# A two-block AdaLN transformer on one core: ScalarE's squares of the projected banks move behind VectorE's two products

## The chip, the cores and the metric

The kernel runs on one core of one Trainium2 chip. The metric is device time in microseconds (us) from the start to the end of one execution, lower is better. The kernel before was run three times: 1238.51, 1242.51 and 1245.01 us, median 1242.51 us.

A core has five engines that run side by side and wait for each other by semaphores: TensorE (PE in the profile, with its weight loads as PEld), VectorE (DVE), ScalarE (ACT), GpSimd (POOL) and SyncE (SP, which here issues DMAs). Each of them works through its own list of instructions in order. TensorE writes its results to PSUM, which has 8 banks of 128 partitions x 512 fp32 numbers; here each matmul result of a step takes one bank.

## The reference

The reference is two blocks of a transformer with adaptive layer norm. The change lies in the last part of the second block, a small "local attention" transformer of two layers on 4 sequences of 1024 tokens with 128 channels, 8 heads of 64. For each layer:

```
h  = shift_token(x)                     # half the channels come from the token before
q, k, v = h @ Wqkv                      # 128 -> 3 x 512, 8 heads of 64
q, k = l2norm(q) * q_scale, l2norm(k) * k_scale      # each head's 64 numbers by their length
q, k = rotary_xpos(q, k)                # x*cos + rotate_half(x)*sin, with a scale by position
a  = softmax(8 * q k^T over the 64 tokens of the window before and the own one)
x  = x + (a v) @ Wo
x  = x + GLU-MLP(layernorm(shift_token(x)))          # 128 -> 2 x 341, gelu, -> 128
```

So for every token and head a length is needed: the root of the sum of 64 squares of q, and the same of k.

## The kernel before, in words

From about 580 us on, the kernel works on the local layers (lines 647 to 1096). Tokens are cut into 64 tiles of 128 (2 layers x 4 sequences x 8 tiles), and one loop goes through them, one step for one tile. In step g the stages of several tiles lie side by side: scores of tile g, projections of tile g+2, transposes of q and k of tile g+1, flips of the probabilities of tile g-2, the products with v of tile g-3, and a piece of the output projection or of the MLP. TensorE's order is written by hand (the loop runs under a manual schedule for PE); for the other engines a tile scheduler orders the instructions from their dependencies and the order of the source text, sets the semaphores, and hands out the buffers of the pools, PSUM's among them: 6 banks in turn for everything of "mid" size, 2 for scores.

One step on PE in order: 32 small matmuls of the scores (L885), projection of q for tile g+2 (L653), the flip of half 0 of tile g-2 (L926), projection of k for tile g+2 (L653), the flip of half 1, the transpose of q of tile g+1 (L845, "turn" with w = 0), the outputs of tile g-3 (L940), the transpose of k of tile g+1 (L845, w = 1), a piece of the MLP, v of tile g-1 (L864), and in one step of four the output projection (L951).

`project` is the function that is changed. It is called twice for a tile, w = 0 for q and w = 1 for k, and each call fills one PSUM bank qk (L653) that three instructions read:

- ScalarE squares it into sq (L656);
- VectorE multiplies it by the cosine table into co (L658);
- VectorE multiplies its swapped halves by the sine table into si (L663).

The framework lets two engines read the same PSUM bank only one after the other, in the order of the source text. Behind them VectorE sums sq over each head into ss (L665, one tile of 16 numbers for q and k together). For w = 1 GpSimd then takes a maximum of ss (L668) and its power -1/2 (L669), adds si to co (L673, for both w), and multiplies the k side by its 1/length (L675). The result is what the transposes (L845) wait for. q's 1/length is used later: VectorE's masking of the scores (L892) takes it as its scale, together with the row minimum. ScalarE's exponentials (L904) follow, eight of them a tile. The division by the sums is done by `over_sums` on tiles of step g-1: a reciprocal (L912) on VectorE, placed behind the copy of the transposed k (L858, kT), then one product for each half (L919), half 0 on GpSimd, half 1 on VectorE. In the MLP pieces, L1004 adds the MLP's result to the stream on VectorE (in the second layer followed by L1006).

Tiles 3 to 7 of the first sequence of the first layer are "light": q's si isn't added on GpSimd, but PE adds it by matmul in the transpose (L849), and half 1's product L919 is done by ScalarE (L917). The first six projections, of tiles 0 to 2, are made earlier, in the last steps of the windowed attention before the local layers (lines 821 and 822).

Of the kernel before, what the change touches and what calls it, by code (L numbers as in the profile page):

```python
# [19 lines left out]
F32 = mybir.dt.float32  # L20
BF16 = mybir.dt.bfloat16
AF = mybir.ActivationFunctionType
# [4 lines left out]
P = 128  # L27
# [9 lines left out]
HEADS, DH, DEPTH = 8, 64, 2  # L37
# [11 lines left out]
def adaln_blocks(ctx: ExitStack, tc: tile.TileContext, a: dict, out: bass.AP):  # L49
    nc = tc.nc  # L50
    pe, act, dve, pool = nc.tensor, nc.scalar, nc.vector, nc.gpsimd
# [11 lines left out]
    def bc(ap, shape):  # L63

        return ap.unsqueeze(len(ap.shape)).to_broadcast(shape)
# [579 lines left out]
    pj = ctx.enter_context(tc.tile_pool(name="pj", bufs=3))  # L645

    def project(l, b, t, w, ps):


        nt = f"{l}_{b}_{t}_{w}"  # L650
        if w == 0:
            late[l, b, t, "ss"] = pj.tile([P, 2, HEADS], F32, tag="ss", name=f"ss_{nt}", bufs=4)
        pe.matmul(ps, lhsT=hs[l, b][:, t * P : (t + 1) * P], rhs=wl[l][0][:, w, :], start=True, stop=True)  # L653
        ph = ps.rearrange("p (h e) -> p h e", e=DH)
        sq = pj.tile([P, HEADS, DH], F32, tag="sq", name=f"sq_{nt}", bufs=2)
        act.activation(sq, ph, AF.Square)  # L656
        co = pj.tile([P, HEADS, DH], F32, tag=f"co{w}", name=f"co_{nt}")
        dve.tensor_tensor(co, ph, abs_[l][:, 0, t, w, :].unsqueeze(1).to_broadcast([P, HEADS, DH]), ALU.mult)  # L658
        si = pj.tile([P, HEADS, DH], F32, tag="si", name=f"si_{nt}", bufs=3)

        ex = bass.AP(tensor=ps.tensor, offset=ps.offset + 32, ap=[ps.ap[0], [DH, HEADS], [-32, 2], [1, 32]])
        sn = abs_[l][:, 1, t, w, :].rearrange("p (i e) -> p i e", i=2).unsqueeze(1).to_broadcast([P, HEADS, 2, 32])
        dve.tensor_tensor(si.rearrange("p h (i e) -> p h i e", i=2), ex, sn, ALU.mult)  # L663
        ss = late[l, b, t, "ss"]
        dve.tensor_reduce(ss[:, w, :], sq, AX.X, ALU.add)  # L665
        if w == 1:

            pool.tensor_scalar(ss, ss, 1.0e-24, None, ALU.max)  # L668
            pool.tensor_tensor(ss, ss, nhalf[:, 0:2].unsqueeze(2).to_broadcast([P, 2, HEADS]), ALU.pow)  # L669
        if w == 0 and light(l, b, t):  # L670
            late[l, b, t, "si"] = si
        else:
            pool.tensor_tensor(co, co, si, ALU.add)  # L673
        if w == 1:
            pool.tensor_tensor(co, co, bc(ss[:, 1, :], [P, HEADS, DH]), ALU.mult)  # L675
        late[l, b, t, "co", w] = co

    def light(l, b, t):

        return (l, b) == (0, 0) and t >= EARLY  # L680
# [5 lines left out]
    with (  # L686
# [107 lines left out]
        for g in range(-1, NG8 + 2):  # L794
            b, t = divmod(g, NT)
            ahead = 0 <= b and b + 1 < B
            if g == -1:
                weights(0, 0)
            when(g + 2, scores)
            when(g + 2, weights)  # L800
            if ahead and t in (2, 4):
                queries(b + 1, t // 2 - 1)
            for after, k, f in ((6, 0, tokens), (8, 0, normed), (11, 1, tokens), (13, 1, normed)):
                if (g - after) % NT == 0 and 0 <= (g - after) // NT < B - 1:
                    f((g - after) // NT, k, "h3")
            for at, k, f in ((1, 0, tokens), (3, 0, normed), (5, 1, tokens), (7, 1, normed)):
                if g == at:
                    f(B - 1, k, "h2")
            when(g - 1, back)
            when(g + 1, flip, (0, 1))  # L810
            when(g + 1, values)
            when(g, outputs)
            when(g + 1, flip, (2, 3))
            if t == 5 and 0 < b <= DEPTH:
                rotary(tab, abs_[b - 1], b - 1)
            if g % 4 == 1 and g > 4:
                project_out((g - 5) // NT, (g - 5) % NT // 4)
            if ahead and t in (3, 5):
                keys(b + 1, t // 2 - 1)

            for i, w in ((0, 0), (0, 1), (1, 0), (1, 1), (2, 0), (2, 1))[max(0, g - NG8 + 6) : max(0, g - NG8 + 7)]:
                project(0, 0, i, w, ps.tile([P, BLK], F32, tag="t", name=f"qk_0_0_{i}_{w}", bufs=2))
# [6 lines left out]
    with (  # L829
# [230 lines left out]
        def project_mid(l, b, t, w):  # L1060
            if (l, b) != (0, 0) or t >= EARLY:
                project(l, b, t, w, pM.tile([P, BLK], F32, tag="mid", name=f"qk_{l}_{b}_{t}_{w}"))
# [161 lines left out]
```

## Time and profile before

| | before |
|---|---|
| three runs, median | 1238.51, 1242.51, 1245.01; 1242.51 us |
| the profiled execution: its time, its span | 1246.33 us, 1244.5 us |
| TensorE clock granted, mean | 0.983 of full speed |
| busy: PE, DVE, ACT, POOL | 1162.8, 878.8, 817.8, 823.3 us |
| the same in the stretch from 800 to 1000 us | 198.49, 173.75, 158.37, 175.65 of 200 us |
| one of the 128 squares (L656, ACT) | 586 ns |
| one cosine product (L658), sine product (L663), head sum (L665), all DVE | 677, 678, 673 ns |
| one add co+si (L673), power (L669), product co*ss (L675), POOL | 1280, 2995, 1044 ns |
| one exponential (L904, ACT), with its accumulator read | 403 + 199 ns, overlapping |
| one masking of a score tile (L892, DVE) | 342 ns |

The durations of an instruction include some overlap with the next of the same engine: in the timeline three VectorE instructions of 0.67 us follow each other every 0.60 us. The busy times are shares of one engine's own time; how long a step takes is read from the start of one block of scores (L885) on PE to the next. The profile's time runs from the span's start.

### The profile page before, as it was taken

To read this page: it belongs to the slowest core of one execution; us is meant where nothing else is said; L and a number is where in the kernel's file an instruction comes from. 1 tells how busy PE (TensorE), PEld (TensorE's weight loads), DVE (VectorE), ACT (ScalarE), POOL (GpSimd) and SP (SyncE) were. 2 spreads that over 40 slices of the span, in tenths; PEclk is the share of its full clock that TensorE was granted. 3 is DMA by queue.
4 is the path that set the end of the run, shared out by engine and by line. 5 is a ranking of instruction groups with operands and counts; after the bars stand their busy time and mean duration, and the time that the engine had idled before them with its cause. 6 is when DMAs were issued, how large, how long until landed. Compare 5 with 4: busy or idle time off the path is not lost.

```text
span 1244.5 us, 34772 instructions
## 1 busy us (share of the span) xinstructions
PE 1162.8 (93%) x13578; PEld 714.7 (57%) x13578; DVE 878.8 (71%) x2798; ACT 817.8 (66%) x2223; POOL 823.3 (66%) x813
## 2 busy tenths in 40 slices
PE   6789999999899999988898999999999999999998
PEld 5644453534476667755665556665555556565564
DVE  5556263452476667666878988898898888998864
ACT  3363373322577677766886788788877887788862
POOL 4436445746334445444889988888899889888840
PEclk8699999999999999999999999999999999999999
DMA  6040404021400000000112111111111111111110
GB/s 179 1 130 8 138 0 132 7 74 63 137 4 4 3 20 14 11 3 3 35 27 48 27 35 26 32 40 27 39 28 34 39 29 45 38 27 31 36 40 26
DMA packets 36136, 51.04 MB, mean 41 GB/s; under 512 B 5850, under 2 KB 17668, under 8 KB 35844
## 3 DMA queue, kind: packets, MB, share of 16 engines
q1 hardware_dynamic: 35540, 48.29, 14.1%
q8 instruction: 107, 1.75, 0.6%
q10 hardware_dynamic: 432, 0.53, 0.1%
q14 instruction: 57, 0.47, 0.1%
HBM read 26.52 MB, written 2.36 MB: 23 GB/s over the span
## 4 chain that ended last, share of the span: by engine, by line
PE 43%; DVE 27%; ACT 18%; POOL 7%; issue 5%; DMA 1%; POOLq 0%; ACTq 0%; SPq 0%; DVEq 0%
ACT pr L904 5%; PE h L489 4%; PE yp L951 4%; DVE pr L892 3%; DVE co L658 3%; PE s L885 3%; DVE si L663 3%; DVE ss L665 3%; PE ptr L735 3%; PE qk L653 3%; POOL u L494 2%; ACT sq L656 2%; PE s L261 2%; PE obank L752 2%; DVE ge L997 2%
## 5 line engine op out<-in xcount | busy, mean ns | idle before, releaser
L904 ACT ACTIVATE pr<-pr,mx 128x128 f32<-128x128 f32 x512 | 200.8, 403 | 88.2 <-DVE mx L892 88.1
L673 POOL TENSOR_TENSOR co<-co,si 128x512 f32<-128x512 f32 x123 | 156.7, 1280 | 79.5 <-DVE si L663 72.2
L669 POOL TENSOR_TENSOR ss<-ss,nhalf 128x16 f32<-128x16 f32 x64 | 191.7, 2995 | 5.3
L892 DVE CUSTOM_DVE_ANT_0 pr<-s,masks,ss 128x128 f32<-128x128 f32 x512 | 144.2, 342 | 42.4 <-PE s L885 42.0
L653 PE MATMUL qk<-wqkv,hs 128*128 128x512 f32 x256 | 137.7, 620 | 4.9 <-ACT pt L737 4.9
L494 POOL TENSOR_TENSOR u<-u,cw 128x512 f32<-128x512 f32 x64 | 81.1, 1271 | 74.4 <-ACT u L492 74.4
L489 PE MATMUL h<-hT,w 128*128 128x512 f32 x256 | 123.8, 605 | 4.0 <-DVE g L496 4.0
L496 DVE TENSOR_TENSOR g<-u,h 128x512 f32<-128x512 f32 x64 | 43.8, 686 | 114.9 <-POOL u L494 114.9
L279 DVE TENSOR_REDUCE mx<-s 128x4 f32<-128x448 f32 x128 | 73.5, 617 | 56.4 <-PE s L270 56.4
L658 DVE TENSOR_TENSOR co<-qk,ab 128x512 f32<-128x512 f32 x128 | 86.7, 677 | 26.0 <-ACT sq L656 26.0
L904 ACT ACTIVATION_READ_ACCUMULATOR pr<-pr,mx 128x1 f32 x512 | 101.7, 199 | 0.0
L492 ACT ACTIVATE u<-h 128x512 f32<-128x512 f32 x64 | 38.2, 598 | 93.2 <-PE h L489 85.7
L926 PEld LDWEIGHTS ptr<-ident,pr 128*128 128x128 f32 x512 | 63.5, 141 | 61.6 <-issue 54.8
L663 DVE TENSOR_TENSOR si<-qk,ab 128x512 f32<-128x512 f32 x128 | 86.8, 678 | 0.0
L489 PEld LDWEIGHTS h<-hT,w 128*128 128x128 f32 x256 | 48.3, 194 | 66.2 <-issue 51.0
L665 DVE TENSOR_REDUCE ss<-sq 128x8 f32<-128x512 f32 x128 | 86.2, 673 | 0.0
L656 ACT ACTIVATE sq<-qk 128x512 f32<-128x512 f32 x128 | 74.9, 586 | 14.8 <-PE qk L653 12.3
L845 PE MATMUL qktr<-ident,co 128*128 128x128 f32 x492 | 76.9, 280 | 6.6 <-POOL co L675 5.3
L885 PEld LDWEIGHTS s<-kT,qT 64*64 64x64 f32 x2048 | 56.8, 134 | 45.6 <-issue 22.1
L919 POOL TENSOR_TENSOR pr<-pr,sm 128x512 f32<-128x512 f32 x64 | 74.7, 1168 | 7.9 <-DVE sm L912 7.9
L885 PE MATMUL s<-kT,qT 64*64 64x128 f32 x2048 | 72.1, 277 | 7.6 <-DVE kT L858 6.1
L737 ACT COPY pt<-ptr 112x512 f32<-112x512 f32 x128 | 72.5, 612 | 8.6 <-PE ptr L735 8.6
(212 smaller groups left out, 2871.2 us busy)
## 6 DMA issues: line engine op xcount, KB each, us to landing
cw<-cd SPq DMA_DIRECT2D x128, 128.0 KB, 3.0
ve<-vs SPq DMA_DIRECT2D x120, 128.0 KB, 2.3
hs<-hT SPq DMA_DIRECT2D x16, 256.0 KB, 3.2
out<-out SPq DMA_DIRECT2D x7, 256.0 KB, 2.7
xin<-in_x SPq DMA_DIRECT2D x3, 512.0 KB, 6.1
w<-in_w SPq DMA_DIRECT2D x3, 512.0 KB, 5.0
wqkv<-in_wqkv SPq DMA_DIRECT2D x2, 768.0 KB, 5.3
ab<-in_tab SPq DMA_DIRECT2D x1, 1024.0 KB, 7.3
```

The lines of the kernel that those rows point to most:

```text
L489: pe.matmul(h, lhsT=w[:, c * P : (c + 1) * P], rhs=hT[b][:, blk(k)], start=True, stop=True)
L494: pool.tensor_tensor(u, u, kept[b, k, "cw"][:, c, :], ALU.mult)
L653: pe.matmul(ps, lhsT=hs[l, b][:, t * P : (t + 1) * P], rhs=wl[l][0][:, w, :], start=True, stop=True)
L656: act.activation(sq, ph, AF.Square)
L658: dve.tensor_tensor(co, ph, abs_[l][:, 0, t, w, :].unsqueeze(1).to_broadcast([P, HEADS, DH]), ALU.mult)
L663: dve.tensor_tensor(si.rearrange("p h (i e) -> p h i e", i=2), ex, sn, ALU.mult)
L665: dve.tensor_reduce(ss[:, w, :], sq, AX.X, ALU.add)
L669: pool.tensor_tensor(ss, ss, nhalf[:, 0:2].unsqueeze(2).to_broadcast([P, 2, HEADS]), ALU.pow)
L673: pool.tensor_tensor(co, co, si, ALU.add)
L885: pe.matmul(S[j][qs, c, :], lhsT=q[rw, c, qs], rhs=k[rw, c, at : at + P], start=True, stop=True)
L892: dve.tensor_tensor_reduce(out=pr[:, c, :], in0=S[j][:, c, :], in1=mk[:, min(t, 1), :], scale=kept[l, b, t, "ss"][:, 0, h : h + 1], scalar ...
L904: act.activation(pr[:, c, :], pr[:, c, :], AF.Exp, bias=mx[:, j, c : c + 1], scale=-1.0, accum_out=sm[:, j, c : c + 1])
```

## The change

Two lines of `project` move: the tile sq and its square on ScalarE are written behind the two products of VectorE instead of ahead of them. Nothing is added and nothing is left out; shapes, pools and buffer counts stay as they are.

```
         pe.matmul(ps, lhsT=hs[l, b][:, t * P : (t + 1) * P], rhs=wl[l][0][:, w, :], start=True, stop=True)
         ph = ps.rearrange("p (h e) -> p h e", e=DH)
-        sq = pj.tile([P, HEADS, DH], F32, tag="sq", name=f"sq_{nt}", bufs=2)
-        act.activation(sq, ph, AF.Square)
         co = pj.tile([P, HEADS, DH], F32, tag=f"co{w}", name=f"co_{nt}")
         dve.tensor_tensor(co, ph, abs_[l][:, 0, t, w, :].unsqueeze(1).to_broadcast([P, HEADS, DH]), ALU.mult)
         si = pj.tile([P, HEADS, DH], F32, tag="si", name=f"si_{nt}", bufs=3)
...
         dve.tensor_tensor(si.rearrange("p h (i e) -> p h i e", i=2), ex, sn, ALU.mult)
+        sq = pj.tile([P, HEADS, DH], F32, tag="sq", name=f"sq_{nt}", bufs=2)
+        act.activation(sq, ph, AF.Square)
         ss = late[l, b, t, "ss"]
         dve.tensor_reduce(ss[:, w, :], sq, AX.X, ALU.add)
```

In the semaphores of the built program this reads, for each of the 128 banks: before, the square waits for PE, the cosine product for the square; after, the cosine product waits for PE, the square for the sine product, and the head sum for the square as before. Since the square of a bank is now its last reader, the next matmul into the same bank waits for the square, and no longer for the sine product.

The scheduler also lays out three engines anew. What most steps hold after the change, in the order of each engine (steps with MLP pieces differ a little):

- ScalarE: the squares come behind the exponentials (exp x3, pt, exp x2, pt, exp x2, square of q, exp, qT, square of k, os), where they came between the first of them.
- VectorE: cosine and sine product of q, then of k, then the head sum of q, kT, the head sum of k, the reciprocal, L919. Before it was cosine, sine, sum of q, cosine, sine, sum of k, kT. In the step in which the MLP's result is added (L1004), that addition too comes ahead of the head sum of k; in the second layer L1006 comes between this sum and the reciprocal.
- GpSimd: L673 twice, L668, L919, L669, L675. Before it was L673 twice, L668, L669, L675, L919. So one product L919 now stands ahead of the power.

PE's order is the same before and after.

More of the change, by code (lines that the diff above doesn't have):

```diff
@@ L654, in project @@
         ph = ps.rearrange("p (h e) -> p h e", e=DH)
-        sq = pj.tile([P, HEADS, DH], F32, tag="sq", name=f"sq_{nt}", bufs=2)
-        act.activation(sq, ph, AF.Square)
         co = pj.tile([P, HEADS, DH], F32, tag=f"co{w}", name=f"co_{nt}")
@@ L663, in project @@
         dve.tensor_tensor(si.rearrange("p h (i e) -> p h i e", i=2), ex, sn, ALU.mult)
+        sq = pj.tile([P, HEADS, DH], F32, tag="sq", name=f"sq_{nt}", bufs=2)
+        act.activation(sq, ph, AF.Square)
         ss = late[l, b, t, "ss"]
```

## Prediction

> **What bounds the kernel now.** I read the page's busy times first, then windows by stage, then the waits inside the stage that changes, then timelines of single steps.
>
> The page's slices (each 31 us; a digit is the busy share in tenths):
>
> ```profile
> PE   6789999999899999988898999999999999999998
> DVE  5556263452476667666878988898898888998864
> POOL 4436445746334445444889988888899889888840
> ```
>
> The changed function works from slice 18 on (its first square starts at 538.2 us, the last at 1179.2). There PE is full. The windows put numbers on it (columns: PE, PEld, DVE, ACT, POOL busy us, granted clock, DMA share, GB/s):
>
> ```profile
> 573.00:640.00 67.00, 58.75 (x747) 40.75 (x749) 54.31 (x194) 50.91 (x182) 49.66 (x40) 0.97 0.11 25
> 700.00:800.00 100.00, 98.25 (x962) 59.06 (x962) 88.68 (x315) 76.74 (x244) 89.40 (x75) 1.00 0.14 32
> 800.00:1000.00 200.00, 198.49 (x1918) 119.61 (x1916) 173.75 (x598) 158.37 (x497) 175.65 (x143) 1.00 0.14 34
> ```
>
> From 800 us on PE lacks 1.51 of 200 us, at full clock. Blocks of scores (L885) begin at 844.55, 853.92, 863.99, 873.72 and 884.38 us: steps of 9.37 (call it A, with Gelu matmuls), 10.07 (B), 9.73 (C, with L1004) and 10.66 us (D, with the output projection), 39.83 for four. So a gain can come only from small PE gaps, while a loss needs only one instruction that comes late for PE. DVE and POOL are at 87%, without much slack.
>
> The waits from 700 to 1100 us (us in total, times, longest) say what the old order cost:
>
> ```profile
> POOL co L673 <- DVE si L663: 38.9, 44, 2.2
> PEld v L864 <- DVE kT L858: 9.3, 10, 1.0
> DVE co L658 <- ACT sq L656: 8.0, 10, 1.0
> ```
>
> DVE waits for a square ten times, about 0.8 us each: once in four steps, in B, where Gelu's table load keeps ACT late. Over the whole run it is 26.0 us in 23 waits, of which PE feels little: the kT copy, last in DVE's queue, holds v back 10 times.
>
> **The change, part by part.** Nothing is added or removed: 128 squares, 256 products and 128 head sums keep their time. Three orders move.
>
> (1) *DVE no longer waits for ACT ahead of the products*, and kT (L858) comes ahead of k's head sum: one 0.60 us instruction less in front of it, and in B the 0.78 us wait gone. What PE can win is only where kT holds it. B: the kT copy starts at 7.89 us into the step; without wait and sum at 7.89 - 0.78 - 0.60 = 6.5, but its transpose (L845) ends only near 7, so about 7.0. v waited 0.93 us for it including PE's usual turnaround; of this I take 0.2 as a gain, as the next bank becomes free only by the square of k. C: scores wait for kT by 0.4 us at the next step's start; kT 0.6 us earlier takes all of it: -0.37. A and D: nothing waits for kT. Together -0.57 us in four steps.
>
> (2) *The head sum of k comes later.* Here C and D matter. C before, on DVE (start, duration; C begins at 903.82):
>
> ```profile
> 911.47 0.68 DVE L663 TENSOR_TENSOR si<-qk,ab 128x512 f32<-128x512 f32 x1
> 912.07 0.67 DVE L665 TENSOR_REDUCE ss<-sq 128x8 f32<-128x512 f32 x1
> 912.67 0.67 DVE L858 COPY kT<-qktr 128x512 f32<-128x512 f32 x1
> 913.26 0.73 DVE L1004 SCALAR_TENSOR_TENSOR hT<-ym,cols,hT 128x512 f32<-128x512 f32 x1
> ```
>
> The sum ends at 912.74, 0.75 us before D begins (913.49). In the new order it is behind kT and L1004: 0.59 + 0.66 = 1.25 us later by start to start, and C itself 0.37 us shorter, so it ends 1.15 us (taken) into D, 1.9 us later against D's start. On POOL, D before:
>
> ```profile
> 910.96 1.49 POOL L919 TENSOR_TENSOR pr<-pr,sm 128x512 f32<-128x512 f32 x1
> 912.58 1.27 POOL L673 TENSOR_TENSOR co<-co,si 128x512 f32<-128x512 f32 x1
> 913.94 0.26 POOL L668 TENSOR_SCALAR ss<-ss 128x16 f32<-128x16 f32 x1
> 914.28 3.34 POOL L669 TENSOR_TENSOR ss<-ss,nhalf 128x16 f32<-128x16 f32 x1
> 917.69 1.04 POOL L675 TENSOR_TENSOR co<-co,ss 128x512 f32<-128x512 f32 x1
> 918.70 1.04 POOL L919 TENSOR_TENSOR pr<-pr,sm 128x512 f32<-128x512 f32 x1
> ```
>
> and what PE then does with L675's result:
>
> ```profile
> 918.83 0.66 PE L845 MATMUL qktr<-ident,co 128*128 128x128 f32 x4
> ```
>
> PE wants it 5.34 us into D; L675 ends there at 5.24 us (one quad earlier, with a power of 2.92 us, at 4.66). It just fits.
>
> (3) *L919 comes ahead of the power on POOL.* In D after the change: head sum ends at 1.15; L668 +0.3; L919 +1.05; power +3.0 (most since 640 us last 2.92 to 2.93, some up to 3.47); L675 +1.05 = 6.6; PE's queue +0.1 = 6.7. PE waits 6.7 - 5.34 = 1.35 us. Without L919 it would be 0.3. In A, B and C the head sum is out before the step ends and L675 would end near 3.9 or earlier, behind which the transpose at about 5.3 doesn't wait: 0, with L919's own 1.05 hidden in POOL's idle 1.5 to 2 us of a step.
>
> L919 is not always 1.04 us. In the trace of before it takes 1.03 to 1.05 us where VectorE's own L919 doesn't run beside it (41 of 57 from 640 us on), and 1.48 to 1.51 us where it does (16). After the change VectorE's L919 directly follows the reciprocal that releases POOL's, so in the first layer they run side by side: +0.45, D's wait 1.8. In the second layer L1006 (0.75 with its overlap) stands between the head sum and the reciprocal, so L919 starts about 0.5 later: 1.85. I take 1.8 for both. The Trainium skill ("SBUF — State Buffer", "Who interferes with whom") states that a VectorE instruction with two SBUF inputs contends with a GpSimd instruction that reads SBUF, the second input coming through a shared interface; the two durations agree. By the rows alone, were no L919 slowed, D's wait would be 1.35 and the sum below 5.4 us smaller.
>
> The waits that didn't exist before, a square behind a sine product and PE behind a square, have no row. From one side 0: in C the sine product of k ends at about 8.4 and ACT, with qT and os done, squares it by 9.0, before DVE asks. From the other side, ACT's squares wait their turn behind 0.48 us copies and 0.39 us exponentials: one copy late is 0.5 us of PE in every step, 2.0 us in four. I take 0, since PE reuses a "mid" bank only six matmul groups later, and keep 2.0 for the range.
>
> The Trainium skill ("PSUM — Partial Sum Buffer", "PSUM bank collisions raise a hardware error") says that two engines may not access one bank and quadrant at once, reads against reads included. Here that is the 26.0 us of DVE behind ACT; the rule means that the three readers can only change places: a bank's three reads stay 0.48 + 0.6 + 0.6 us in a row, and by it alone the change would be worth 0.
>
> *Light steps* (g = 3 to 6, 609.62 to 635.32): 9.33 and 8.57 us each, PE waiting 0.37 to 0.52 us for kT at the start of scores, and L675 done at 614.13 where its transpose comes at 616.31. kT moves up, L675 keeps cover: 4 x -0.47 = -1.9. *Start* (538 to 600 us): the squares of the first tiles come behind whole tiles of exponentials, so tile 3's L675, for which PE already waits 3.0 us at 597.95, comes later by 0.3 to 2 us, with up to 0.45 won earlier: taken +1.0, bounds -0.5 and +2. Steps g = 8 to 11 have POOL-set gaps that move from one step to the next: 0.
>
> **The sum.** Four steps: +1.8 - 0.05 (the 0.37 that D loses of PE's turnaround can hide in the wait) - 0.57 = +1.18. L1004 comes 12 times with such a head sum behind it: 12 x 1.18 = +14.2; -1.9; +1.0; total +13.3 on the profiled execution's 1246.33 us, so 1259.6. The median of the runs shown is 1242.51, 0.9969 of it: 1255.8. Since the 1.8 is at the long end of (2) and (3) (1.35 gives 1250), I forecast **1254 us, +0.9%**.
>
> **Rivals.**
>
> *The late head sum finds cover (faster).* The scheduler's order is that of issue, and if the head sum of k in C ends 1.5 us earlier than I laid it (L1004 is late for nothing and DVE has gained 0.6 to 0.8 in the steps before), L675 ends by 5.3 and only (1) is left: 12 x -0.57 - 1.9 = -8.7: 1237.6, or 1234 on the median. For: DVE is 13% idle, and it stops waiting in B. Against: L919 ahead of the power is a fixed 1.05 to 1.5 us that no DVE slack takes away; it alone fills the 0.1 to 0.7 us of slack in D. It decides where L675 ends under 5.3 us into D.
>
> *It cancels (within 0.5%).* D's wait is 0.6 to 0.9, for example since the next steps, whose PE gaps are 0.4 each, give it back: about +0 to +0.3 in four steps, -1.9 + 1.0: 1241 to 1245.
>
> *Banks come free late (slower by more).* PE waits for squares in most steps at 0.5 us each: 12 x 2.0 = +24 on top: 1283.6, 1280 on the median. For: a square now ends a bank, and ACT is the engine whose queue holds eight exponentials. Against: six banks. Half of it gives 1267.
>
> **How the numbers follow.** The measurement can tell about 0.5% (6.2 us) from no change. Chances: forecast (1249 to 1261) 0.42, cancels 0.2, faster 0.22, banks late 0.16. That gives slower 0.58, same 0.2, faster 0.22. The range takes in the faster rival's 1234 and half of the late banks: 1233 to 1268.
>
> **What would show it.** Right: steps of 9.37, about 9.85, 9.35 and 12.4; PE idle at L845 in D put to POOL L675, about 1.8 us, 12 times; POOL's L919 mostly near 1.5 us, ahead of L669; the wait of DVE co for ACT sq gone, and DVE ss waiting for ACT sq in its place, small. Wrong: D stays near 10.7 (faster rival), or PE or PEld rows that wait for ACT sq with over 10 us in sum (late banks), or a changed gap at 598 us by more than 2 us.

## The result, and the profile after

The changed kernel takes 1251.57 us (median of 6 runs, 1250.0 to 1253.69); the kernel before, with further runs, 1242.06 us (median of 6). The ratio is 1.008, 95% interval 1.006 to 1.0099: slower by 0.8%. The profiled execution has 1253.69 us and a span of 1251.9 us.

The slices of the page lie as before; what changed is seen in the windows (PE, PEld, DVE, ACT, POOL busy, clock, DMA share, GB/s):

```profile
700.00:800.00 100.00, 95.76 (x945) 58.56 (x935) 88.71 (x309) 76.66 (x242) 87.62 (x73) 1.00 0.14 32
800.00:1000.00 200.00, 193.40 (x1861) 115.76 (x1860) 171.99 (x579) 152.45 (x470) 170.25 (x138) 1.00 0.14 33
```

PE lacks 6.6 of 200 us where it lacked 1.5, at the same clock. The groups of the page (busy us, mean ns | idle before, releaser) say what it now waits for and what became slower. (In the changed kernel the cosine product is L656, the sine product L661 and the square L663; the other line numbers used here are the same in both.)

```profile
L845 PE MATMUL qktr<-ident,co 128*128 128x128 f32 x492 | 76.9, 280 | 23.2 <-POOL co L675 22.3
L665 DVE TENSOR_REDUCE ss<-sq 128x8 f32<-128x512 f32 x128 | 87.1, 681 | 14.2 <-ACT sq L663 12.3
L919 POOL TENSOR_TENSOR pr<-pr,sm 128x512 f32<-128x512 f32 x64 | 85.0, 1329 | 7.5 <-DVE sm L912 7.5
```

In the kernel before, two of these rows read:

```profile
L845 PE MATMUL qktr<-ident,co 128*128 128x128 f32 x492 | 76.9, 280 | 6.6 <-POOL co L675 5.3
L919 POOL TENSOR_TENSOR pr<-pr,sm 128x512 f32<-128x512 f32 x64 | 74.7, 1168 | 7.9 <-DVE sm L912 7.9
```

The transposes L845 waited 5.3 us for GpSimd's L675 before, now 22.3. The head sum waits for the square (before, the cosine product did, for 26.0 us). L919 on GpSimd takes 1329 ns in the mean, before 1168. The waits from 700 to 1100 us:

```profile
PEld qktr L845 <- POOL co L675: 14.3, 10, 1.7
PE qktr L845 <- POOL co L675: 12.9, 10, 1.6
PEld a L995 <- ACT sq L663: 10.9, 18, 0.9
```

Of the ten waits of PE, seven are in D steps of the first layer, where the transpose comes 1.6 us late, two in D steps of the second (0.7 us), and one in step 16 (0.4 us). The third row is new too: the MLP's second and third matmul, in B, wait for a bank that a square now ends. Their weights waited about as long before, 10.0 us in the same stretch, 5.6 of them for a bank that the sine product ended. Step C and D of the quad shown before, after the change, on VectorE (D begins at 915.13 us):

```profile
913.80 0.67 DVE L661 TENSOR_TENSOR si<-qk,ab 128x512 f32<-128x512 f32 x1
914.40 0.68 DVE L858 COPY kT<-qktr 128x512 f32<-128x512 f32 x1
914.99 0.73 DVE L1004 SCALAR_TENSOR_TENSOR hT<-ym,cols,hT 128x512 f32<-128x512 f32 x1
915.65 0.67 DVE L665 TENSOR_REDUCE ss<-sq 128x8 f32<-128x512 f32 x1
916.25 0.18 DVE L912 RECIPROCAL sm<-sm 128x8 f32<-128x8 f32 x1
916.47 0.69 DVE L919 TENSOR_TENSOR pr<-pr,sm 128x512 f32<-128x512 f32 x1
```

on GpSimd:

```profile
916.41 0.26 POOL L668 TENSOR_SCALAR ss<-ss 128x16 f32<-128x16 f32 x1 [0.52 <-DVE ss L665]
916.63 1.43 POOL L919 TENSOR_TENSOR pr<-pr,sm 128x512 f32<-128x512 f32 x1
918.02 2.92 POOL L669 TENSOR_TENSOR ss<-ss,nhalf 128x16 f32<-128x16 f32 x1
921.02 1.04 POOL L675 TENSOR_TENSOR co<-co,ss 128x512 f32<-128x512 f32 x1
```

and on PE:

```profile
922.11 0.66 PE L845 MATMUL qktr<-ident,co 128*128 128x128 f32 x4 [1.57 <-POOL co L675]
```

The head sum is behind kT and L1004 and ends 1.2 us into D; L919 stands ahead of the power and runs beside VectorE's L919, 1.43 us instead of 1.04; L675 ends 6.93 us into D, where the transpose could start at 5.34.

By stages, from the starts of the scores' blocks (us of the profiled executions):

| stage | before | after | difference |
|---|---|---|---|
| first projection to the first scores block | 44.25 | 43.80 | -0.45 |
| steps 0 to 2 | 19.02 | 18.59 | -0.43 |
| light steps 3 to 6 | 35.04 | 33.87 | -1.17 |
| steps 7 to 18 | 118.96 | 119.87 | +0.91 |
| A, eleven of them | 9.37 or 9.80 each | the same | 0 |
| B, eleven | 10.07 to 10.12 | 9.95 to 10.00 | -1.4 |
| C, ten | 9.66 to 9.74 | 9.47 to 9.55 | -1.9 |
| D in the first layer, seven | 10.66 | 12.30 | +11.5 |
| D in the second layer, four | 10.76 or 11.20 | 11.47 or 11.91 | +2.8 |

That is +9.9 us. The -0.45 of the first row is no gain that can be told from scatter: in the traces of the eight kernels of this document that have the new order throughout the first sequence, this stage takes between 43.59 and 44.86 us. In steps 7 to 18 the same thing as in D is seen: in steps 7, 9, 12 and 16 L919 stands ahead of the power, L675 ends 6.11, 6.34, 6.76 and 5.80 us into the step, and PE waits 0.75, 0.98, 1.41 and 0.44 us for it at L845. The profiled span grew by 7.4 only, since the first projection came 2.5 us earlier in this execution, in code that the change doesn't touch.

### The profile page after: what moved, and what is told of

Its sections match the earlier page's. It is cut to its first block, busy times and chain, and to the rows that moved or that the text cites. A ratio compares the mean times of both kernels' runs of the same rounds, so it can differ in the third digit from the quotient of the medians.

```text
span 1251.9 us, 34775 instructions
## 1 busy us (share of the span) xinstructions
PE 1160.1 (93%) x13578; PEld 714.7 (57%) x13578; DVE 894.6 (71%) x2798; ACT 820.8 (66%) x2223; POOL 825.5 (66%) x813
## 4 chain that ended last, share of the span: by engine, by line
DVE 17%; ACT 16%; PE 15%; POOL 7%; issue 2%; DMA 0%; ACTq 0%; POOLq 0%; DVEq 0%
ACT pr L904 6%; PE yp L951 4%; POOL ss L669 3%; DVE pr L892 3%; DVE ss L665 3%; ACT sq L663 2%; ACT pt L928 2%; DVE ge L997 2%; PE s L885 2%; ACT ge L990 2%; DVE si L661 2%; DVE co L656 2%; DVE pr L919 1%; PE v L864 1%; POOL pr L919 1%
## 5 line engine op out<-in xcount | busy, mean ns | idle before, releaser
L673 POOL TENSOR_TENSOR co<-co,si 128x512 f32<-128x512 f32 x123 | 155.6, 1277 | 64.8 <-DVE si L661 60.0
L669 POOL TENSOR_TENSOR ss<-ss,nhalf 128x16 f32<-128x16 f32 x64 | 187.0, 2921 | 2.6
L845 PE MATMUL qktr<-ident,co 128*128 128x128 f32 x492 | 76.9, 280 | 23.2 <-POOL co L675 22.3
L904 ACT ACTIVATION_READ_ACCUMULATOR pr<-pr,mx 128x1 f32 x512 | 98.1, 192 | 0.0
L665 DVE TENSOR_REDUCE ss<-sq 128x8 f32<-128x512 f32 x128 | 87.1, 681 | 14.2 <-ACT sq L663 12.3
L656 DVE TENSOR_TENSOR co<-qk,ab 128x512 f32<-128x512 f32 x128 | 86.7, 677 | 10.3 <-PE qk L653 10.3
L919 POOL TENSOR_TENSOR pr<-pr,sm 128x512 f32<-128x512 f32 x64 | 85.0, 1329 | 7.5 <-DVE sm L912 7.5
L663 ACT ACTIVATE sq<-qk 128x512 f32<-128x512 f32 x128 | 75.7, 591 | 21.2 <-DVE si L661 18.2
L661 DVE TENSOR_TENSOR si<-qk,ab 128x512 f32<-128x512 f32 x128 | 86.8, 678 | 0.0
L701 POOL COPY hr<-hT 128x384 f32<-128x384 f32 (+1 forms) x32 | 15.5, 484 | 95.3 <-PE vp L710 95.3
```

What stands on the lines that cost most here:

```text
L904: act.activation(pr[:, c, :], pr[:, c, :], AF.Exp, bias=mx[:, j, c : c + 1], scale=-1.0, accum_out=sm[:, j, c : c + 1])
L919: eng.tensor_tensor(pr, pr, bc(sm[:, j, :], [P, 4, P]), ALU.mult)
```

## The experiments

**The theory** after the result: D waits for L675, because the head sum of k is late (behind kT and L1004) and L919 stands ahead of the power. **Rival 1**: banks come free late, since squares end them. **Rival 2**: only one of the two parts of the theory counts. Ratios are to the kernel before on the same chip, with 95% intervals.

**1. GpSimd's product held behind the power.**

```diff
-            pool.tensor_tensor(co, co, bc(ss[:, 1, :], [P, HEADS, DH]), ALU.mult)
+            late["scaled"] = pool.tensor_tensor(co, co, bc(ss[:, 1, :], [P, HEADS, DH]), ALU.mult)
...
-            with tc.issue_after(kept["copied"].ins):
+            with tc.issue_after(kept["copied"].ins), tc.issue_after(kept["scaled"].ins):
```

> The changed kernel, with GpSimd's product L919 held behind L675 again (behind the power), all else as changed. Main theory (PE waits in step D for L675, which is late by the late head sum of k and by the product L919 ahead of the power): first-layer D steps fall from 12.30 us by about the 1.43 us of that product, to 10.9 to 11.3; second-layer D steps, where the product stands behind already, stay at 11.47 and 11.91; in all 8 to 10 us less than the changed kernel, 1241 to 1244. Rival 1 (banks that come free late by the squares): the order on GpSimd doesn't matter, 1251 +- 2. Rival 2 (only the head sum counts, the product would have found room): 1249 to 1252.

Measured: ratio 0.9993 (0.9979 to 1.0006), so the whole loss of the total is gone; first-layer D 11.31 us, second-layer D unchanged at 11.47 and 11.91. What D still loses (7.4 us in all) is met by what B, C and the steps up to 18 gain (1.4, 1.9 and 2.7 us). Rival 1 alone falls. The 1.43 us of the product give back only 0.99 in D, and GpSimd's rows of that kernel say why:

```profile
910.70 0.26 POOL L668 TENSOR_SCALAR ss<-ss 128x16 f32<-128x16 f32 x1 [0.51 <-DVE ss L665]
911.03 3.19 POOL L669 TENSOR_TENSOR ss<-ss,nhalf 128x16 f32<-128x16 f32 x1
914.30 1.04 POOL L675 TENSOR_TENSOR co<-co,ss 128x512 f32<-128x512 f32 x1
```

Now it is the power that begins while VectorE's L919 runs, and takes 3.19 instead of 2.92 us.

**2. L1004 held behind the head sum of k.**

```diff
-        dve.tensor_reduce(ss[:, w, :], sq, AX.X, ALU.add)
+        late["sum"] = dve.tensor_reduce(ss[:, w, :], sq, AX.X, ALU.add)
...
+            with tc.issue_after(kept["sum"].ins):
+                dve.scalar_tensor_tensor(yT[b][:, s], y, cols[:, V_B2 + l : V_B2 + l + 1], yT[b][:, s], ALU.add, ALU.add)
```

> The changed kernel, with the MLP's addition L1004 (and L1006) on VectorE held behind the head sum of k; the product L919 stays ahead of the power in the first layer. Main theory: the sum of k ends 0.5 to 0.66 us earlier in every D step, so the L675 wait shrinks by as much: first-layer D 11.65 to 11.8, second-layer D 10.8 to 11.0, in all 6 to 8 us less than the changed kernel, 1244 to 1246. Rival 1 (late banks): 1251 +- 2. Rival 2 (only the product ahead of the power counts): first layer unchanged at 12.3, 1249 to 1251.

Measured: 1.0091 (1.0078 to 1.0104), no gain. The sum ended 0.45 us earlier against D's start, and first-layer D fell to 11.92; but the scheduler now placed the reciprocal ahead of the sum, and so L919 ahead of L668 in both layers: second-layer D rose by 0.78, to 12.25 and 12.69. A miss in the total, and a second sight of what the product costs there: ahead of the power, 0.78 more in spite of the earlier sum.

**3. Both held.** Edits 1 and 2 together.

> The changed kernel with both undone that the main theory blames: GpSimd's product L919 behind the power, and L1004 (with L1006) behind the head sum of k. Main theory: in D the sum ends 0.75 us into the step, L668 0.3, power 2.9 to 3.2, L675 1.05: 5.3 to 5.5 us where PE wants it at 5.34; first-layer D steps 10.7 to 10.9, second-layer D 10.8 and 11.2, the gains of 0.1 in B and 0.2 in C and about 1 each at the start and in the light steps kept: 3 to 6 us less than the kernel before on the same chip, ratio 0.995 to 0.998. Rival 1 (late banks): still slower than before, 1.002 to 1.006, since all squares end their banks.

Measured: 1.0006 (0.999 to 1.0023): not the gain expected. L675 ends 5.25 us into D, in time, and the transposes don't wait; still D takes 11.11, and 11.77 and 12.20. PE's rows by line show the next in the queue:

```profile
L845 PE MATMUL qktr<-ident,co 128*128 128x128 f32 x492 | 77.3, 281 | 4.8 <-POOL co L675 3.9 <-DVE xT L771 0.9
L864 PE MATMUL v<-wqkv,hs 128*128 128x512 f32 x128 | 68.0, 613 | 6.0 <-ACT sq L663 4.7 <-ACT qT L852 1.4
```

The wait moved from L845 to v (L864), whose bank the square of q ends 6.57 us into D, behind seven exponentials. Rival 1 is true, but stood behind the longer wait for L675.

**4 and 5. The new order for one of the two banks.** Here 4; in 5 the two conditions are exchanged.

```diff
+        if w == 1:
+            act.activation(sq, ph, AF.Square)
...
+        if not (w == 1):
+            act.activation(sq, ph, AF.Square)
         ss = late[l, b, t, "ss"]
```

> The new order for the bank of q alone; the bank of k is squared first as before. In the built program the head sum of k then stands ahead of L1004 and the product L919 behind L675 in all steps. Main theory: no late L675, D steps of 10.7 to 10.9; the wait of VectorE in B is mostly kept or moved to the product of k; in all 1238 to 1243, like the kernel before or a little less. Rival 1 (late banks): half of the squares still end their bank, so half of the loss stays, 1246 to 1248.

Measured for q alone: 1.0234 (1.0218 to 1.0249), far off. The scheduler put kT and L919 ahead of q's head sum, and all of k's three instructions behind it, so the head sum of k ends as late as in the changed kernel (1.09 us into D), and GpSimd's product L675 ran beside VectorE's L919:

```profile
928.10 2.92 POOL L672 TENSOR_TENSOR ss<-ss,nhalf 128x16 f32<-128x16 f32 x1
931.11 1.52 POOL L678 TENSOR_TENSOR co<-co,ss 128x512 f32<-128x512 f32 x1
```

(L672 and L678 are that kernel's power and L675.) First-layer D 12.2 to 12.4, second-layer 13.1 and 13.4, B 10.4, light steps 9.09. My reading of the built order (sum ahead of L1004, so early) overlooked what had come ahead of k's products.

> The new order for the bank of k alone; the bank of q is squared first as before. In the built program the head sum of k is behind kT and L1004 as in the changed kernel, and L919 ahead of the maximum and the power. Main theory: first-layer D about 12.3 as in the changed kernel, second-layer D over 11.5, B's wait of VectorE for the square of q kept, C 9.5: 8 to 14 us more than the kernel before on the same chip, ratio 1.006 to 1.011. Rival 1 (late banks): half of the squares end their bank, half of the loss, ratio about 1.004.

Measured for k alone: 1.004 (1.0021 to 1.0059). First-layer D 11.70, C 9.37, B 10.36. First-layer D goes in the direction expected, and less far, since the sum ended 0.59 and not 1.2 us into D; second-layer D, 10.89 and 11.31, missed its expectation. The total is the 1.004 that rival 1 gave, and in part for its reason: B is 0.29 longer, 3.1 us in all, and there the MLP's matmul and its weights wait for a bank that the square of k ends (800 to 1100 us):

```profile
PEld a L998 <- ACT sq L666: 8.4, 7, 1.2
PE a L998 <- ACT sq L666: 2.6, 7, 0.4
```

(L998 and L666 are that kernel's matmul and late square.) The seven first-layer D steps cost 7.3 us, with L675 late, and C gives back 3.3.

**6. The product ahead in the squares-first kernel.** L668, L669 and L675 of the tiles with t % 4 == 0 (but for the first sequence of the first layer) are written after the product of the next step and issued behind it.

```diff
+            def finish():
+                with tc.issue_after(late["half0"].ins) if "half0" in late else ExitStack():
+                    pool.tensor_scalar(ss, ss, 1.0e-24, None, ALU.max)
+                    pool.tensor_tensor(ss, ss, nhalf[:, 0:2].unsqueeze(2).to_broadcast([P, 2, HEADS]), ALU.pow)
+                    pool.tensor_tensor(co, co, bc(ss[:, 1, :], [P, HEADS, DH]), ALU.mult)
...
             when(g - 1, over_sums)
+            kept.pop("finish", lambda: None)()
```

`half0` is GpSimd's product L919.

> The kernel before, squares first, with one difference: in the D steps GpSimd's product L919 is put ahead of the maximum and the power. VectorE's order is untouched, so the head sum is early. Main theory: the reciprocal is ready 0.5 us into D, the product takes 1.04 to 1.5, power and L675 end near 6.4 us into D where PE wants them at 5.34: about 1.0 us more in each of some 13 D steps, 1253 to 1257. Rival 2 (only the late head sum counts): 1242 to 1244. Rival 1 (late banks): 1242 to 1243, since no square has moved.

Measured: 1.0238 (1.0216 to 1.026), 28.8 us more on the same chip, far over the 1253 to 1257 us expected. D is 12.07 in the first layer (+1.4) and 12.36 and 12.80 in the second (+1.6), 16 us in eleven steps, with an early sum and no square moved. The other 12.7 us lie in steps 11 and 15 (+4.1, +8.6), where my edit made the power wait for a product that itself came late; they say nothing on the change. In the D steps that the run was made for, about 1.0 us was expected.

**7 and 8. The late sum in the squares-first kernel.** For the tiles projected in C, the head sum of k (and what follows from it) is issued behind L1004; in 8 with edit 1 as well.

```diff
+            add = dve.scalar_tensor_tensor(yT[b][:, s], y, cols[:, V_B2 + l : V_B2 + l + 1], yT[b][:, s], ALU.add, ALU.add)
+            if "finish" in kept:
+                with tc.issue_after(add.ins):
+                    kept.pop("finish")()
```

`finish` holds the head sum, L668, L669 and L675.

> The kernel before, squares first, with one thing of the change put in by hand: in the C steps (12 tiles) the head sum of k is issued behind kT and L1004. The scheduler then puts the product L919 ahead of the power in D of its own accord, as in the changed kernel. Main theory: first-layer D 12.1 to 12.3, second-layer D about 11.5 and 11.9, C 9.4 to 9.5, B and the light steps as before: 10 to 14 us more than the kernel before on the same chip, ratio 1.008 to 1.012. Rival 1 (late banks): no square has moved, ratio 0.998 to 1.002.

> As the run with the late sum in the squares-first kernel, with the product L919 held behind L675. Main theory: D steps about 11.3 in the first layer and 11.5 and 11.9 in the second as in the changed kernel with that product behind, C 9.4 to 9.5: 4 to 7 us more than the kernel before on the same chip, ratio 1.003 to 1.006. If the late sum alone were harmless and only the product counted: ratio 0.997 to 1.000.

Measured: 1.0082 (1.006 to 1.0104) and 1.0026 (1.0009 to 1.0043). With the sum late, the scheduler put L919 ahead of the power by itself, as in the changed kernel: first-layer D 11.92 to 11.99, second-layer 11.17 and 11.55, C 9.37. Held behind, first-layer D 10.93 to 10.99. Step 11 is 4.6 and 3.3 us longer, step 15 1.0: with the sum held by hand, GpSimd does work of the layer norm first, and L675 ends 8.23 us into step 11 where it ended at 6.61. The changed kernel has no such loss there (step 11 takes 11.51), so the ratios overstate; the step lengths are the result. So the loss in D is had without moving a square, from the late sum alone, and in the first layer some three quarters of it from what the scheduler does with the late sum.

**What ties 1 to 8 together** is when L675 ends in D (read from the timeline of one quad in the first layer, us from D's start), against the length of that D:

| kernel | head sum of k ends | L675 ends | D |
|---|---|---|---|
| before | -0.75 | 5.25 | 10.66 |
| changed | 1.20 | 6.93 | 12.30 |
| 1, product behind | 1.19 | 5.93 | 11.31 |
| 2, L1004 behind | 0.76 | 6.56 | 11.92 |
| 3, both behind | 0.76 | 5.25 | 11.11 |
| 4, q only | 1.09 | 6.86 | 12.23 |
| 5, k only | 0.59 | 6.33 | 11.70 |
| 6, before, product ahead | -0.75 | 6.71 | 12.08 |
| 7, before, late sum | 0.81 | 6.55 | 11.92 |
| 8, the same, product behind | 0.82 | 5.56 | 10.93 |

All but kernel 3 lie within 0.02 us of D = 10.66 + (L675's end - 5.29), where that is positive. Kernel 3 is the one with a different last wait.

**9 to 11. Versions for use.** In all three, the tiles of the first sequence of the first layer have the new order and L919 is held behind L675. From the others, 10 has the old order, with the head sum of k in C between kT and L1004 (from step 18 on); 9 is the same with the new order for the tiles projected in B; 11 has the new order for those projected in A and B and no moved sum.

```diff
+        new = (l, b) == (0, 0) or t % 4 == 3
+        if not new:
+            act.activation(sq, ph, AF.Square)
...
+        if new:
+            act.activation(sq, ph, AF.Square)
...
+        hold = True and w == 1 and (l * B + b) * NT + t >= 20 and t % 4 == 0
...
                 when(g + 1, turn, 1)
+            if "finish" in kept:
+                with tc.issue_after(kept["copied"].ins):
+                    kept.pop("finish")()
```

This is 9. In 10 `new` has only its first part; in 11 it has t % 4 in (2, 3), and `hold` is never true. Edit 2 is in all three.

> A version for use, from what the runs showed: the new order only for the eight tiles of the first sequence of the first layer; all others squares first as before, but in the C steps from step 18 on the head sum of k stands behind kT and ahead of L1004, and the product L919 is held behind L675. Main theory (two places where the new order costs: the head sum behind L1004 in C, and PE waiting for a bank that a square ends in D): C 9.37, D 10.66 to 10.75, start and light steps as in the changed kernel with the product behind (2.5 us less up to step 10): 5 to 7 us less than the kernel before on the same chip, ratio 0.994 to 0.997. If the kT gain in C is given back in D: about 2 us less, 0.998.

> As the run with the sum between kT and L1004, and in addition the new order for the tiles projected in B steps (t % 4 == 3), where VectorE waited 0.78 us for the square. Main theory: B falls from 10.07 to about 9.95, since both banks are changed there, so 1.3 us less in all than that run, ratio 0.993 to 0.996. Rival 1 (late banks): B stays or grows to 10.3, since a step later a bank ended by a square is waited for: the same or up to 3 us more than that run.

> The new order for all tiles but those projected in C and D steps; the product L919 behind L675 everywhere, the head sum ahead of kT in C as before. Main theory: A 9.37, B 9.95, C 9.67 and D 10.66 as before, start and light steps improved by 2.5 us: 3 to 4 us less than the kernel before on the same chip, ratio 0.997. Rival 1 (late banks in A and B too): D or A grow, ratio 1.000 or more.

Measured: 10: 0.9962 (0.9944 to 0.9979); 9: 0.993 (0.9911 to 0.9949); 11: 0.9966 (0.9946 to 0.9987). In 9 the steps are 9.37, 9.96, 9.37 and 10.66 in the first layer, and the window has PE busy throughout:

```profile
800.00:1000.00 200.00, 200.00 (x1937) 120.85 (x1937) 175.48 (x613) 160.25 (x500) 176.29 (x143) 1.00 0.15 34
```

Second-layer D is 11.03 and 11.40, 0.2 to 0.3 over before. Kernel 9 beats both kernels: 1237.95 us, where the kernel before took 1245.28 on the same chip, 7.3 us less. Its steps account for 4.2 of these (C -3.3, B -1.3, second-layer D +0.9, steps 11 to 18 -0.7, steps 0 to 10 +0.2); where the rest lies was not found. It isn't in the first projections: the stretch up to the first scores takes 44.59 us in its trace, 0.3 more than before. In the fourteen traces the first projection itself starts anywhere from 529.1 to 538.3 us, behind code that no edit touches, so a few us between two profiled executions lie there. In 10, B stays at 10.07 and C is 9.37; in 11, C is 9.56 to 9.64 and no D is longer than before.

**12. What held up kernel 3.** Kernel 3 with the tiles projected in D squared first (but for the first sequence of the first layer).

```diff
+        new = (l, b) == (0, 0) or t % 4 != 1
```

> The run with L919 and L1004 both held behind (L675 on time, yet D 11.11 and 11.77 to 12.20 us, with PE's v waiting for a square), and in addition the tiles projected in D (t % 4 == 1) squared first as before. If the rest of D's loss is the bank that a square ends late: first-layer D 10.66 to 10.75, second-layer D 10.9 to 11.5, no wait of v for the square; B 9.95 and C 9.5 kept: 4 to 6 us less than that run, ratio to the kernel before 0.995 to 0.998. If the rest comes from L1004 and L919 standing ahead of the masks on VectorE in D: D stays at 11.1 and 11.8, ratio 1.000 to 1.001.

Measured: 0.998 (0.9963 to 0.9996). First-layer D 10.86, second-layer 11.52 and 11.96: between the two theories. v no longer waits; from 800 to 1180 us the next wait in D is

```profile
PEld yp L962 <- DVE si L665: 9.5, 9, 1.4
```

(L962 and L665 are that kernel's output projection and sine product; in the kernel before this wait was 4.1 us in ten times). The masks begin 1.93 us into D there, before at 1.29, and the sine product of k 6.49 instead of 5.85. So of the 0.45 us that kernel 3 lost in first-layer D, 0.25 was the bank that a square ended, and 0.2 the products that come later because L1004 and VectorE's L919 stand ahead of the masks.

## Why the prediction was right, point by point

The forecast was 1254 us, +0.9%, and the result is 1251.57, +0.8%. The mechanism was the one forecast, in the place forecast, and also in steps 7, 9, 12 and 16, where it was put at nothing. Several sizes were off and cancelled in part, so the closeness of the two numbers is in part luck. From one profiled execution to the other, the sum was +13.3 and the stages above show +9.9: D's term was +21.0 and is +13.6, the gains of B and C were 6.8 and are 3.5, that of the light steps 1.9 and is 1.2, the start was +1.0 and is -0.9, and the other steps from 7 to 17, put at 0, are +1.8.

- *(2) and (3), the wait in D, first layer*: 12.4 was forecast, 12.30 measured, with the sum at 1.2 (1.15 forecast), the product at 1.43 beside VectorE's L919 (1.49) and L675's end at 6.93. The 1.15 was itself a lucky value. The working (1.25 later, C shorter by 0.37, the sum at -0.75) gives 0.87, and the rest was taken without a reason. Measured, C is only 0.19 shorter, and the sine product of k comes 0.50 us later in C (8.15 us into the step instead of 7.65), behind the head sum of q and a VectorE L919 of 1.32 us, which (1) had not seen. That the product ahead of the power is the larger part was shown by 1 and 6, that the late sum alone calls it forth by 7.
- *(3), second layer*: 1.85 was worked out and 1.8 taken, 0.71 measured in each. The failed step is "so L919 starts about 0.5 later: 1.85". With the reciprocal behind L1006, the scheduler put L919 behind the power in those steps; in kernel 2, where the reciprocal came ahead of the sum, L919 stood ahead in the second layer too. I had taken one step's order for all. This oversized the sum by 4.4 us.
- *The count of D*: 12 were forecast. Eleven had the loss; the first, step 15, became 0.69 shorter. That oversized the sum by some 2 us.
- *(1), kT*: B -0.2 forecast, -0.12 measured; C -0.37 forecast, -0.19 measured. In C kT still came behind VectorE's L919 (1.32 us beside GpSimd's, 0.71 before). In 7, where the old order of products stood and the sum came behind kT, C gave 0.30 to 0.37 (9.37).
- *Light steps*: -1.9 forecast, -1.17 measured. (The stretch given, 609.62 to 635.32, is that of steps 4 to 6; step 3 begins at 600.29.) In steps 4 to 6 kT was copied 0.23 us earlier, not 0.47: the sine product of k waited behind the head sum of q, which now waited for its square.
- *Start*: +1.0 forecast, bounds -0.5 to +2; measured -0.9, outside the bounds, of which -0.43 in steps 0 to 2 and -0.45 ahead of them, where it is within scatter. The squares did come later, but the wait for tile 3 at 598 us was 2.57 instead of 3.00 us.
- *The rival "banks come free late"*: taken as 0, kept as 2.0 us in four steps. It is there and smaller: in D 0.25 us, covered by the wait for L675 and seen only when that is gone (3 and 12). In B the weights of the MLP's matmuls wait 10.9 us for squares in 400 us, where they waited 10.0 before, and B is still shorter. With the bank of k alone (5) it made B 0.29 longer.
- *The rival "the late head sum finds cover"*: fell. In no run with the product ahead of the power did L675 end under 6.3 us in a D from step 19 on.
- *The slowed L919*: SBUF's shared interface (the Trainium skill, "SBUF — State Buffer", "Who interferes with whom") agrees with 1.43 against 1.04 us, and with the power's 3.19 against 2.92. But running side by side is not enough, as the prediction had it: two of its 41 short L919 had VectorE's beside them, begun later (see the last section).

## What to carry to other kernels

When an instruction is moved back on a full in-order engine, look at its last consumer several engines on: here a head sum of 0.6 us, late by 2 us, had no slack through a 3 us power on GpSimd, and PE paid. A scheduler answers a late input with a new order of other queues, and that answer can cost more than the delay, so the built order of each kind of step has to be read, not one of them. Where steps differ, an order can be chosen by step: the new order in the steps that gain and the old one in those that lose, together with queue orders held by hand, was worth 0.7%, where the change for all lost 0.8%.

## What the runs showed that was not expected

- GpSimd's power (L669), whose inputs are tiny, is slowed too by a VectorE product with both inputs in SBUF: 3.19 us against 2.92, and L675 1.52 against 1.04 in kernel 4. What counts is which of the two began first. In kernel 1 VectorE's product began 0.28 us ahead of the power of 3.19 us shown there:

```profile
910.75 0.69 DVE L919 TENSOR_TENSOR pr<-pr,sm 128x512 f32<-128x512 f32 x1
```

In kernel 3 the power began 0.14 us ahead of it, and neither took longer than alone:

```profile
871.93 2.92 POOL L669 TENSOR_TENSOR ss<-ss,nhalf 128x16 f32<-128x16 f32 x1
872.07 0.68 DVE L919 TENSOR_TENSOR pr<-pr,sm 128x512 f32<-128x512 f32 x1
```

From 640 us on, all fourteen traces agree: the 147 powers that began while VectorE's L919 or L1006 ran took 3.19 to 3.47 us, the 51 during which one began later took 2.92 or 2.93, like those with none. So holding one GpSimd instruction away from that product hands the cost to the next only if the next begins while the product runs.
- An order that ends a bank with a square cost nothing that could be seen while PE waited elsewhere, and became the last wait as soon as that was mended (kernel 3: v, 4.7 us in PE's row).
- With PE busy 198.5 of 200 us in the kernel before, there was still 0.7% to be had (0.5 to 0.9), of which the steps show 0.3 us in each C and 0.1 in each B.
